# A four-layer hybrid kernel: first image requested ahead of the weights, first chunk's entry with one transfer behind its last step, first head's keys requested beside the last convolution

## The chip, the core and the metric

The kernel runs on one core of one Trainium2 chip. A core has five engines that run side by side, each through its own list of instructions in order: TensorE (PE in the profile, with its weight loads shown apart as PEld), VectorE (DVE), ScalarE (ACT), GpSimd (POOL) and SyncE (SP), which here issues nearly all transfers. The transfers themselves run on 16 DMA engines. The metric is the device time of one execution in microseconds (us), as the median of several runs; lower is better.

## The reference

The input x is four images of 128 channels by 64 x 64 pixels, in fp32. Four layers follow, each added to its input.

```python
x = x + _L0_conv_ref(_gn(x), ...)      # group norm, two depthwise convolutions, a patch sort, a scan
x = x + _L1_conv_ref(_gn(x), weight, bias)   # group norm, a 3x3 convolution of 128 to 128 channels
t = _to_tokens(x)                      # 4096 tokens of 128 channels per image
t = t + _L2_attn_ref(_ln_t(t), ...)    # attention with 16 heads of 8, then a small feed-forward
t = t + _L2_ffn_ref(_ln_t(t), ...)     # 64 experts
t = t + _L3_attn_ref(_ln_t(t), ...)    # linear attention
t = t + _L3_ffn_ref(_ln_t(t), ...)     # 64 experts
```

Layer 0 is what most of the change touches. Its core, for one image:

```python
feat = _gelu(_dwconv2d(x, conv1_w)); feat = feat * channel_gate(feat)
feat = _gelu(_dwconv2d(feat, conv2_w))
order = argsort of a score per 4x4 patch            # 256 patches
x1 = x[order] + pe[order];  x1n = layernorm(x1)     # 4096 positions in sorted order
xm, z = split(x1n @ in_proj_w.T)
xc = silu(causal convolution of 4 taps over xm)
dt = softplus(low-rank projection of xc)
h[t] = exp(dt * A) * h[t-1] + dt * B[t] * xc[t];  y[t] = sum over 16 states of h * C[t]
out = ((y + D * xc) * silu(z)) @ out_proj_w.T, put back at the original positions
```

In layer 2's attention the queries and keys of a head are the same 8 numbers, products of cosines of the normalised tokens, and the softmax runs over all 4096 tokens.

## The kernel before

**Layers 0 and 1** are written in `layers01` (line 284). It begins by requesting all weights on SP: eight small columns and matrices, then z_projT, conv1d_b, dt_projT, dt_b, the eight strided pieces of A_log, d_skip, out_projT, taps (the weights of layer 1), bias, x_projT, in_projT and taps1d, and the six pieces of the depthwise weights (`deep_t`). Some small products of weights follow on DVE and ACT, among them `taps1d * in_projT` (line 349) and `a_neg = -exp(A_log)` (lines 352 and 353).

`in_order(b)` (line 440) then prepares one image: it loads the image in four parts (`image`, line 397), takes the group norm's statistics (`groupnorm_scale`, line 177), writes the normalised image with a border into `xp`, stores `xp` to DRAM, and gathers it back in the layout that the depthwise convolution needs, eight rows at a time (`gather`, line 462: three transfers into a tile `under`, of which there are two). The first convolution's result `fp` is stored and gathered in the same way for the second. Scores per patch are sorted into ranks, the position rows `pe` are requested and added, each chunk of 512 positions is centred into `xn`, and `scaled_by_root` (line 678) multiplies it by the inverse deviation: TensorE spreads the deviations into PSUM, ACT copies them to `rs`, and POOL multiplies the two halves. Transposes and products with a permutation matrix give the sorted sequence `xq`.

For image 0 this runs alone (line 1050), in numbered slots: a slot is one step of the generator, and `K.slot` is its number. Outside the scan and the attention stages, a planner sets the order of each engine's instructions: it simulates the engines and, whenever one comes free, gives it the earliest-written instruction whose inputs and buffer are ready.

`scan` (line 736) walks over the four images in 32 chunks of 512 positions; its order is written out by hand for all engines, SP included. `enter(n)` (line 754) prepares chunk n while chunk n-1 is scanned. It computes xc, the projections and dt; `twice` (line 815) sends a tile through four transfers so that each 64 channels stand on both halves of the partitions. The last steps before the change are POOL's `e - u`, POOL's `dt + e`, `twice(dt2, dt)`, POOL's `dtx = dt * xc` and `twice(dtx2, dtx)`. Chunk 0's entry runs alone, before the scan's first step. Beside the scan of one image, `in_order` of the next image runs; beside the last, layer 0's end and layer 1 for the first three images. An operation given to `later` is issued at the next `K.flush`.

After the scan, `last()` (line 1084) does layer 0's end and layer 1 for image 3: `put_back`, group norm, and the 3x3 convolution in 16 pieces, some 50 steps.

**Layer 2** (`layer2_attention`, line 1128) has for each image a `prepare` (line 1243): eight chunks of 512 tokens through six stages (`fetch`, `centred`, `norm`, `products`, `running`, `store`), 48 steps; `store` writes the head values to `head_d` and `value_d` in DRAM. `loads` (line 1331) then asks for the keys and queries of head 0 with 32 transfers from `head_d` and casts both on POOL. `attention` (line 1344) follows, with the order on PE, DVE and POOL written by hand. For image 0, `prepare` runs step for step beside `last()`, and the loads run after both:

```python
part, l0_pools = before
run(part, stages)
l0_pools.close()
two = open_(left, "l2_two", 2)
run(loads(two))
```

`run` (line 1123) takes one step from each of its parts in turn until all are done. For images 1 to 3, `run(one_by_one(stages, loads(two)), *feed_forward(...))` (line 1728) already runs the loads behind `prepare`, beside the feed-forward of the image before. SBUF pools are opened from two ends, `left` and `right`, like stacks.

**Layers 2 and 3's experts and layer 3's attention** come after and are not touched.

Of the kernel before, what the change touches and what calls it, by code (L numbers as in the profile page):

```python
# [17 lines left out]
P = 128  # L18
NB = 4
# [264 lines left out]
def layers01(K, xd, dpool, w, w1):  # L284
# [14 lines left out]

    norm_g = column(nc, cst, w["norm_g"], "norm_g")  # L300
# [8 lines left out]
    z_projT = matrix(nc, cst, w["in_proj_wT"][:, 256:512], "z_projT")  # L309
    conv1d_b = column(nc, cst, w["conv1d_b"], "conv1d_b", 2)  # L310
    dt_projT = matrix(nc, cst, w["dt_proj_wT"], "dt_projT")
    dt_b = column(nc, cst, w["dt_proj_b"], "dt_b", 2)

    a_neg = cst.tile([P, NQ, NG], F32, name="a_neg")
    for z in range(2):
        for q in range(NQ):
            nc.sync.dma_start(
                out=a_neg[64 * z : 64 * z + 64, q, :].unsqueeze(2),
                in_=w["A_log"][64 * q : 64 * q + 64, :].rearrange("d (g z) -> d g z", z=2)[:, :, z : z + 1],
            )  # L320
    d_skip = column(nc, cst, w["D"], "d_skip", 2)
    out_projT = matrix(nc, cst, w["out_proj_wT"], "out_projT", 2)
    taps = cst.tile([P, 9, P], F32, name="taps")
    nc.sync.dma_start(out=taps, in_=w1["weightT"])
    bias = column(nc, cst, w1["bias"], "bias")

    x_projT = cst.tile([P, 2, 80], F32, name="x_projT")
    nc.vector.memset(x_projT, 0.0)
    for at, rows_ in ((0, slice(0, 24)), (64, slice(24, 40))):
        nc.sync.dma_start(  # L330
            out=x_projT[:, :, at : at + rows_.stop - rows_.start],
            in_=w["x_proj_wT"].rearrange("(k p) f -> p k f", k=2)[:, :, rows_],
        )

# [10 lines left out]
    in_projT = small.tile([P, 256], F32, name="in_projT", tag="rank_eq")  # L345
    nc.sync.dma_start(out=in_projT, in_=w["in_proj_wT"][:, 0:256])
    taps1d = cst.tile([P, 4, 256], F32, name="taps1d")
    nc.sync.dma_start(out=taps1d, in_=w["conv1d_wT"].partition_broadcast(P))
    nc.vector.tensor_tensor(
        taps1d, taps1d, in_projT.unsqueeze(1).to_broadcast([P, 4, 256]), ALU.mult  # L350
    )
    nc.scalar.activation(a_neg, a_neg, AF.Exp)
    nc.vector.tensor_scalar(a_neg, a_neg, -1.0, None, ALU.mult)
# [43 lines left out]
    def image(b):  # L397
        t = big.tile([P, L], F32, name="xb", tag="mid")
        src = w["x"][b].rearrange("c h w -> c (h w)")
        for q in range(4):  # L400
            at = slice(q * L // 4, (q + 1) * L // 4)
            nc.sync.dma_start(out=t[:, at], in_=src[:, at])
        return t

# [35 lines left out]
    def in_order(b, made, work, psum):  # L440
# [3 lines left out]
        xb = image(b)  # L444
# [17 lines left out]
        def gather(i, c):  # L462
            n = 8 * (HW + 2)
            t = unders[c] = work.tile([96, 4, n], F32, name="under", bufs=2)
            for ky in range(3):
                at = (8 * c + ky) * (HW + 2)
                nc.sync.dma_start(
                    out=t[32 * ky : 32 * ky + 32],
                    in_=image_d[i][:, at : at + n].rearrange("(g q) f -> q g f", q=32),
                )  # L470
# [207 lines left out]
        def scaled_by_root(n):  # L678
# [5 lines left out]
            def taken():  # L684
                rs = work.tile([P, CH], F32, name="ln_rs", tag="rs", bufs=1)
# [50 lines left out]
    def scan(seqs, others, work, psum, psbc, psex, psy):  # L736
# [17 lines left out]
        def enter(n):  # L754
# [49 lines left out]
            dt2, dtx2 = (work.tile([P, NQ, CH], F32, name=name) for name in ("dt2", "dtx2"))  # L804

# [16 lines left out]

            yield
# [7 lines left out]
            later(nc.gpsimd.tensor_tensor, e, e, u, ALU.subtract)  # L831
            yield
            later(nc.gpsimd.tensor_tensor, dt, dt, e, ALU.add)
# [1374 lines left out]
```

## Time and profile before

| | |
|---|---|
| median of 3 runs | 9565.78 us (9564.62 to 9581.03) |
| profiled execution | 9578.96 us, span of its instructions 9577.2 us |
| busy share of the span | PE 90%, DVE 75%, ACT 76%, POOL 52% |
| TensorE's mean granted clock | 0.934 of full speed |
| image 0's first scan begins | 234.82 us |
| scan of four images ends | about 2637 us |
| first score of image 0's attention | 2824.01 us |

The profile's times count from the start of the span. "L402" is line 402 of the kernel. A timeline row gives start, duration, engine, line, operation, the tile written and the tiles read, and how many instructions are merged in the row; in brackets stands how long the engine had idled before it and what released it. "SPq" rows are SP's requests for transfers; their duration is that of the issuing, not of the transfer. In a table of windows, each row gives the busy time of the engines in one stretch, TensorE's granted clock, the mean busy share of the 16 DMA engines and the rate in GB/s. An idle engine costs nothing unless what it waits for lies on the path that sets the end.

### The profile page before, as it was taken

What the parts mean: (1) busy time and instruction counts of PE and PEld (TensorE: products, weight loads), DVE (VectorE), ACT (ScalarE), POOL (GpSimd) and SP (SyncE); (2) the same over time, 40 slices, a digit from 0 to 9 for tenths busy, and PEclk for the clock granted to TensorE, in tenths of its full rate; (3) what the DMA queues carried; (4) which work ended last, traced back from release to release, by engine and by line L of the source; (5) the groups of instructions that cost most, each with busy time, mean ns of one, the idle gap of its engine ahead of it and who ended that gap; (6) DMA issues with size and microseconds to landing.
All of it is one profiled execution on the core that took longest, in us unless ns stands there. A gap on an engine that the chain in (4) does not pass through costs nothing.

```text
span 9577.2 us, 189161 instructions
## 1 busy us (share of the span) xinstructions
PE 8608.8 (90%) x74394; PEld 3287.8 (34%) x74394; DVE 7159.3 (75%) x7845; ACT 7287.0 (76%) x10505; POOL 4933.0 (52%) x3287
## 2 busy tenths in 40 slices
PE   5887888889879999979999979999989999998787
PEld 2221222234443333333333333333333333334444
DVE  1889798987858888868888867888876888874464
ACT  3776767654449999969999969999978999984232
POOL 1677676765525555555555545555555555543011
PEclk8887888889989999989999989999989999999998
DMA  4434425222232221141222233221222222231205
GB/s 118 122 77 109 108 72 128 74 67 80 71 86 39 39 41 40 32 112 40 40 40 40 39 94 55 38 41 39 39 81 62 40 40 40 40 97 58 81 10 168
DMA packets 580323, 631.22 MB, mean 66 GB/s; under 512 B 118816, under 2 KB 374888, under 8 KB 578536
## 3 DMA queue, kind: packets, MB, share of 16 engines
q1 hardware_dynamic: 579432, 619.12, 27.5%
q8 instruction: 586, 9.60, 0.4%
q14 instruction: 305, 2.50, 0.1%
HBM read 444.74 MB, written 106.97 MB: 58 GB/s over the span
## 4 chain that ended last, share of the span: by engine, by line
PE 60%; DVE 4%; DMA 2%; POOL 2%; issue 2%; ACT 2%; SPq 0%; DVEq 0%; POOLq 0%; ACTq 0%
PE ctx_ps L92 27%; PE acc_ps L92 14%; PE score L92 12%; PE ln_xc L92 1%; DMA w<-in_L_ffn_weight 1%; PE hid_ps L92 1%; PE kv L92 1%; POOL ln_sd L1845 1%; PE ln_var L129 1%; DVE ctx L1498 0%; DMA queries<-head_d 0%; POOL q L1293 0%; PE pool L92 0%; DVE x L1998 0%; ACT hid L1685 0%
## 5 line engine op out<-in xcount | busy, mean ns | idle before, releaser
L1564 ACT ACTIVATE ex<-score 128x1024 f32<-128x1024 f32 x5120 | 4924.1, 1038 | 235.8 <-PE score L92 147.9
L92 PE MATMUL ctx_ps<-ex,qt 128*32 128x512 f32 x20480 | 2733.2, 606 | 19.7 <-DVE ctx L1498 19.7
L1513 POOL TENSOR_TENSOR folded<-ex 128x1024 f32<-128x1024 f32 x512 | 1223.3, 2389 | 2100.3 <-ACT ex L1564 1826.9
L1570 DVE STREAM_TRANSPOSE turned<-ex 128x1024 f32<-128x1024 f32 x1536 | 1885.3, 1227 | 337.1 <-ACT ex L1564 336.8
L1546 DVE STREAM_TRANSPOSE turned<-ex 128x1024 f32<-128x1024 f32 x1532 | 1841.9, 1202 | 0.0
L92 PE MATMUL acc_ps<-turned,turned_v 128*32 128x256 f32 x24576 | 1769.3, 379 | 3.0 <-POOL qt L1251 2.3
L926 DVE TENSOR_TENSOR_SCAN hs<-decay,carry,hs 128x512 f32<-128x512 f32 x1024 | 1245.4, 1265 | 196.9 <-ACT decay L922 183.8
L92 PE MATMUL score<-queries,keys 32*128 32x512 f32 x10240 | 1334.3, 497 | 51.9 <-POOL queries L1241 47.0
L92 PEld LDWEIGHTS acc_ps<-turned,turned_v 128*32 128x32 f32 x24576 | 800.8, 110 | 1476.6 <-issue 1324.4
L930 POOL TENSOR_TENSOR hs<-hs,c_sb 128x1024 f32<-128x1024 f32 x512 | 1207.0, 2357 | 70.4 <-DMA c_sb<-c_d 31.4
L922 ACT ACTIVATE decay<-dt,a_neg 128x512 f32<-128x512 f32 x1024 | 693.0, 689 | 659.8 <-DVE hs L926 649.8
L92 PEld LDWEIGHTS score<-queries,keys 32*128 32x128 f32 x10240 | 512.4, 182 | 1145.7 <-ACT ex L1564 777.7
L1370 POOL TENSOR_TENSOR turned_v<-v,quarter 128x1024 f32<-128x1024 f32 x256 | 612.9, 2395 | 264.8 <-PE acc_ps L92 222.5
L92 PE MATMUL y_ps<-hs,pair 128*64 128x512 f32 x2048 | 656.1, 769 | 32.2 <-POOL hs L930 32.2
L1514 POOL TENSOR_TENSOR quarters<-folded 128x512 f32<-128x512 f32 x512 | 657.6, 1284 | 40.1
L92 PEld LDWEIGHTS ctx_ps<-ex,qt 128*32 128x32 f32 x20480 | 406.4, 108 | 655.2 <-issue 599.1
L915 DVE TENSOR_TENSOR hs<-dtx,b_ps 128x2048 f32<-128x2048 f32 x256 | 579.8, 2265 | 54.9 <-PE b_ps L92 31.0
L92 PE MATMUL b_ps<-dbc,state 32*64 32x512 f32 x1024 | 340.8, 747 | 237.4 <-DVE hs L915 237.3
L929 POOL COPY carry<-hs 128x2 f32<-128x2 f32 x512 | 97.9, 191 | 688.3 <-DVE hs L926 659.6
L1564 ACT ACTIVATION_READ_ACCUMULATOR ex<-score 128x1 f32 x2048 | 439.0, 214 | 0.0
L1498 DVE COPY ctx<-ctx_ps 128x512 f32<-128x512 f32 x256 | 176.8, 691 | 329.3 <-PE ctx_ps L92 317.8
L1555 DVE TENSOR_REDUCE dacc<-quarters 128x2 f32<-128x512 f32 x508 | 326.9, 643 | 0.0
(376 smaller groups left out, 8785.0 us busy)
## 6 DMA issues: line engine op xcount, KB each, us to landing
c_sb<-c_d SPq DMA_DIRECT2D x512, 128.0 KB
keys<-head_d SPq DMA_DIRECT2D x1024, 64.0 KB
queries<-head_d SPq DMA_DIRECT2D x1024, 64.0 KB
under<-image_d SPq DMA_DIRECT2D x192, 264.0 KB
dt<-dt SPq DMA_DIRECT2D x128, 256.0 KB
dtx<-dtx SPq DMA_DIRECT2D x128, 256.0 KB
v<-value_d SPq DMA_DIRECT2D x1024, 32.0 KB
w<-in_L_ffn_weight SPq DMA_DIRECT2D x32, 1024.0 KB
```

The source lines that it names most:

```text
L92: self.nc.tensor.matmul(out, lhsT, rhs, start=start, stop=stop)
L915: nc.vector.tensor_tensor(hs, dtx2, bb.unsqueeze(1).to_broadcast([P, NQ, CH]), ALU.mult)
L922: nc.scalar.activation(ex, dt2[:, q, :], AF.Exp, scale=a_neg[:, q, g : g + 1])
L926: nc.vector.tensor_tensor_scan(hs[:, q, :], decays[q - 2 * i], hs[:, q, :], carry[:, g, q : q + 1], ALU.mult, ALU.add)
L930: nc.gpsimd.tensor_tensor(hs[:, two, :], hs[:, two, :], cs.unsqueeze(1).to_broadcast([P, 2, CH]), ALU.mult)
L1370: nc.gpsimd.tensor_tensor(t, v.unsqueeze(2).to_broadcast([P, 4 * BT, 4, HD]), quarter.unsqueeze(1).to_broadcast([P, 4 * BT, 4, HD]), ALU.mult,
L1513: nc.gpsimd.tensor_tensor(hs, exs[:, :, 0], exs[:, :, 1], ALU.add)
L1514: nc.gpsimd.tensor_tensor(qs, hs[:, :, 0 : CH // 2], hs[:, :, CH // 2 :], ALU.add)
L1546: nc.vector.transpose(*upright)
L1555: nc.vector.tensor_reduce(at, qs, AX.X, ALU.add)
L1564: nc.scalar.activation(ex, sps[p], AF.Exp, scale=scale, accum_out=sums[:, t : t + 1] if summed else None)
L1570: nc.vector.transpose(*upright)
```

## The change

It has six parts, in the order of the program.

- Image 0 is requested first of all, before any weight. Twelve weights' loads (20 transfers) and their products move from the beginning into image 0's `in_order`, after slot 34; the exponential and negation of `a_neg` are written after slot 84.
- For image 0, `under` has four buffers in place of two.
- For image 0, `scaled_by_root` multiplies with two DVE operations straight from PSUM; the ACT copy and the two POOL products are gone.
- For chunk 0, `dtx2` is first filled with `xc` by `twice`; the two small POOL steps run on DVE; and once `dt2` has arrived, four DVE products make `dtx2 = dtx2 * dt2` in place. The second `twice` at the end is gone.
- `prepare` has two `x_in` buffers in place of three for image 0.
- The pool of keys and queries is opened on the right side, before `prepare`, for images 0 to 3. For image 0 the loads are put behind `prepare`'s stages, and this sequence takes two steps for each step of `last()`.

```diff
+    def image(b):
+        t = big.tile([P, L], F32, name="xb", tag="mid")
...
+    images = {0: image(0)}
+
     norm_g = column(nc, cst, w["norm_g"], "norm_g")
...
-    z_projT = matrix(nc, cst, w["in_proj_wT"][:, 256:512], "z_projT")
-    conv1d_b = column(nc, cst, w["conv1d_b"], "conv1d_b", 2)
-    dt_projT = matrix(nc, cst, w["dt_proj_wT"], "dt_projT")
...
-    nc.scalar.activation(a_neg, a_neg, AF.Exp)
-    nc.vector.tensor_scalar(a_neg, a_neg, -1.0, None, ALU.mult)
...
-        xb = image(b)
+        xb = images.pop(b) if b in images else image(b)
...
-            t = unders[c] = work.tile([96, 4, n], F32, name="under", bufs=2)
+            t = unders[c] = work.tile([96, 4, n], F32, name="under", bufs=2 if b else 4)
...
             def taken():
+                if b == 0:
+                    for a in range(2):
+                        nc.vector.tensor_tensor(inner(n, a), inner(n, a), outer(bp, a), ALU.mult)
+                    return
                 rs = work.tile([P, CH], F32, name="ln_rs", tag="rs", bufs=1)
...
+            light = nc.gpsimd if n else nc.vector
...
+            if n == 0:
+                twice(dtx2, xc)
             yield
...
-            later(nc.gpsimd.tensor_tensor, e, e, u, ALU.subtract)
-            yield
-            later(nc.gpsimd.tensor_tensor, dt, dt, e, ALU.add)
+            later(light.tensor_tensor, e, e, u, ALU.subtract)
+            yield
+            later(light.tensor_tensor, dt, dt, e, ALU.add)
             later(twice, dt2, dt)
             yield
-            later(nc.gpsimd.tensor_tensor, dtx, dt, xc, ALU.mult)
-            later(twice, dtx2, dtx)
+            if n:
+                later(nc.gpsimd.tensor_tensor, dtx, dt, xc, ALU.mult)
+                later(twice, dtx2, dtx)
+            else:
+                for q in range(NQ):
+                    later(nc.vector.tensor_tensor, dtx2[:, q], dtx2[:, q], dt2[:, q], ALU.mult)
...
-        for K.slot, _ in enumerate(in_order(0, seqs, work, psum)):
+        turns = enumerate(in_order(0, seqs, work, psum))
+        for K.slot, _ in turns:
             K.flush()
+            if K.slot == 34:
+                break
+        z_projT = matrix(nc, cst, w["in_proj_wT"][:, 256:512], "z_projT")
...
+        for K.slot, _ in turns:
+            K.flush()
+            if K.slot == 84:
+                nc.scalar.activation(a_neg, a_neg, AF.Exp)
+                nc.vector.tensor_scalar(a_neg, a_neg, -1.0, None, ALU.mult)
         K.flush()
...
-                xs[c] = work.tile([P, CH], F32, name="x_in", bufs=3)
+                xs[c] = work.tile([P, CH], F32, name="x_in", bufs=3 if b else 2)
...
-                if b == NB:
+                if b < NB:
+                    two = open_(right, "l2_two", 2, side="right")
+                else:
                     xs = images()
...
-                        run(part, stages)
+                        stages = one_by_one(stages, loads(two))
+                        run(part, stages, stages)
                         l0_pools.close()
-                        two = open_(left, "l2_two", 2)
-                        run(loads(two))
                     elif b < NB:
-                        two = open_(left, "l2_two", 2)
                         run(one_by_one(stages, loads(two)), *feed_forward(b - 1, past, work, psum))
```

More of the change, by code (lines that the diff above doesn't have):

```diff
@@ L298, in layers01 @@
     small = pool("l0_small", 1)
+    def image(b):
+        t = big.tile([P, L], F32, name="xb", tag="mid")
+        src = w["x"][b].rearrange("c h w -> c (h w)")
+        for q in range(4):
+            at = slice(q * L // 4, (q + 1) * L // 4)
+            nc.sync.dma_start(out=t[:, at], in_=src[:, at])
+        return t
+    images = {0: image(0)}
     norm_g = column(nc, cst, w["norm_g"], "norm_g")
@@ L308, in layers01 @@
     nc.vector.tensor_scalar(head_b, head_b, 0.5, None, ALU.mult)
-    z_projT = matrix(nc, cst, w["in_proj_wT"][:, 256:512], "z_projT")
-    conv1d_b = column(nc, cst, w["conv1d_b"], "conv1d_b", 2)
-    dt_projT = matrix(nc, cst, w["dt_proj_wT"], "dt_projT")
[L312 to L333, printed above, removed]
     row32 = K.shifted("row32_0", K.row_i, 1, (31, None, ALU.bitwise_and))
@@ L343, in layers01 @@
     nc.vector.tensor_tensor(pair, K.ident[:, 0:64], K.ident[:, 64:128], ALU.add)
[L345 to L351, printed above, removed]
-    nc.scalar.activation(a_neg, a_neg, AF.Exp)
-    nc.vector.tensor_scalar(a_neg, a_neg, -1.0, None, ALU.mult)
     head_bc = cst.tile([P, 64], F32, name="head_bc")
@@ L395, in layers01 @@
         nc.vector.tensor_scalar(befores[h], K.col, K.row[:, h : h + 1], None, ALU.is_gt)
[L397 to L403, printed above, removed]
     def staged(n, period, *stages):
@@ L1049, in layers01 @@
     ):
-        for K.slot, _ in enumerate(in_order(0, seqs, work, psum)):
+        turns = enumerate(in_order(0, seqs, work, psum))
+        for K.slot, _ in turns:
             K.flush()
+            if K.slot == 34:
+                break
+        z_projT = matrix(nc, cst, w["in_proj_wT"][:, 256:512], "z_projT")
+        conv1d_b = column(nc, cst, w["conv1d_b"], "conv1d_b", 2)
+        dt_projT = matrix(nc, cst, w["dt_proj_wT"], "dt_projT")
+        dt_b = column(nc, cst, w["dt_proj_b"], "dt_b", 2)
+        a_neg = cst.tile([P, NQ, NG], F32, name="a_neg")
+        for z in range(2):
+            for q in range(NQ):
+                nc.sync.dma_start(
+                    out=a_neg[64 * z : 64 * z + 64, q, :].unsqueeze(2),
+                    in_=w["A_log"][64 * q : 64 * q + 64, :].rearrange("d (g z) -> d g z", z=2)[:, :, z : z + 1],
+                )
+        d_skip = column(nc, cst, w["D"], "d_skip", 2)
+        out_projT = matrix(nc, cst, w["out_proj_wT"], "out_projT", 2)
+        taps = cst.tile([P, 9, P], F32, name="taps")
+        nc.sync.dma_start(out=taps, in_=w1["weightT"])
+        bias = column(nc, cst, w1["bias"], "bias")
+        x_projT = cst.tile([P, 2, 80], F32, name="x_projT")
+        nc.vector.memset(x_projT, 0.0)
+        for at, rows_ in ((0, slice(0, 24)), (64, slice(24, 40))):
+            nc.sync.dma_start(
+                out=x_projT[:, :, at : at + rows_.stop - rows_.start],
+                in_=w["x_proj_wT"].rearrange("(k p) f -> p k f", k=2)[:, :, rows_],
+            )
+        in_projT = small.tile([P, 256], F32, name="in_projT", tag="rank_eq")
+        nc.sync.dma_start(out=in_projT, in_=w["in_proj_wT"][:, 0:256])
+        taps1d = cst.tile([P, 4, 256], F32, name="taps1d")
+        nc.sync.dma_start(out=taps1d, in_=w["conv1d_wT"].partition_broadcast(P))
+        nc.vector.tensor_tensor(
+            taps1d, taps1d, in_projT.unsqueeze(1).to_broadcast([P, 4, 256]), ALU.mult
+        )
+        for K.slot, _ in turns:
[3 more added lines that the diff above has]
+                nc.vector.tensor_scalar(a_neg, a_neg, -1.0, None, ALU.mult)
         K.flush()
```

## The prediction

> **What bounds the kernel now.** I read the page first. TensorE is busy 90% of the span and makes 60% of the chain that ended last, nearly all of that in the attention stages (ctx_ps, acc_ps, score), which the change does not edit. So whatever it brings must come from stretches where no engine is full. I looked for those with the table of windows: the head of the program, before the scan, and the gap between the scan and the first attention. (Below: the chain's shares by engine; then stretch and length, busy us and count of PE, PEld, DVE, ACT, POOL, granted clock, DMA share, GB/s.)
>
> ```profile
> PE 60%; DVE 4%; DMA 2%; POOL 2%; issue 2%; ACT 2%; SPq 0%; DVEq 0%; POOLq 0%; ACTq 0%
> ...
> 10.00:20.00 10.00, 0.00 (x0) 0.00 (x0) 0.61 (x6) 2.80 (x3) 0.00 (x0) 1.00 0.66 142
> ...
> 2790.00:2810.00 20.00, 0.00 (x0) 0.00 (x0) 0.00 (x0) 0.00 (x0) 1.89 (x1) 0.53 0.62 66
> ```
>
> In both windows all compute engines are nearly still while DMA runs. The timeline says what they wait for (start, duration, engine, line, operation; in brackets the idle time and its releaser):
>
> ```profile
> 19.62 2.39 SPq L402 DMA_DIRECT2D xb<-in_x  x4
> 23.37 1.29 DVE L183 BATCH_NORM_STATS2 gn_st<-xb 128x6 f32<-128x512 f32 x2 [0.42 <-DMA xb<-in_x]
> 33.75 5.75 ACT L230 ACTIVATE xp<-xb,gn_off,gn_rs 128x512 f32<-128x512 f32 x8 [0.43 <-DVE gn_off L215]
> 35.33 4.51 SPq L458 DMA_DIRECT2D image_d<-xp  x4
> 46.84 8.72 PE L92 MATMUL conv<-under,deep 96*32 96x512 f32 x48 [13.82 <-DMA under<-image_d]
> 58.16 2.78 PE L92 MATMUL conv<-under,deep 96*32 96x512 f32 x24 [2.60 <-DMA under<-image_d]
> 90.64 4.73 PE L92 MATMUL conv<-under,deep 96*32 96x512 f32 x24 [2.33 <-DMA under<-image_d]
> ```
>
> The image is requested only at 19.62, behind every weight, and the chain (statistics, normalised image, store, gather, convolution) starts there. The first convolution then stalls between gathers.
>
> ```profile
> 172.10 1.66 POOL L691 TENSOR_TENSOR xn<-xn,ln_rs 128x256 f32<-128x256 f32 x2 [0.69 <-ACT ln_rs L686]
> 173.81 1.54 PE L716 MATMUL perm_t<-ident,xn 128*128 128x128 f32 x6 [8.96 <-POOL xn L691]
> ...
> 213.73 1.22 DVE L144 TENSOR_TENSOR dt<-sp_u,dt 128x1024 f32<-128x1024 f32 x1 [22.04 <-ACT dt L144]
> 220.61 2.95 SPq L818 DMA_DIRECT2D dt<-dt  x4
> 223.66 3.46 SPq L818 DMA_DIRECT2D dtx<-dtx  x4
> 232.43 2.29 DVE L915 TENSOR_TENSOR hs<-dtx,b_ps 128x2048 f32<-128x2048 f32 x1 [16.71 <-DMA dtx<-dtx]
> ```
>
> Here two serial chains: rows scaled by an ACT copy and two POOL products a chunk, and the first chunk's entry, which ends in two transfers one behind the other; the scan starts at 234.82.
>
> ```profile
> 2780.75 0.38 SPq L1323 DMA_DIRECT2D head_d<-part  x1
> 2787.78 11.97 SPq L1233 DMA_DIRECT2D keys<-head_d  x16
> 2800.19 15.15 SPq L1233 DMA_DIRECT2D queries<-head_d  x16
> 2822.06 1.89 POOL L1241 CAST queries<-queries 128x2048 fp32r<-128x2048 f32 x1 [12.25 <-DMA v<-value_d]
> 2824.01 1.51 PE L92 MATMUL score<-queries,keys 32*128 32x512 f32 x6 [37.30 <-POOL queries L1241]
> ```
>
> The last convolution ends at 2786.7 and TensorE idles 37.30 us for 32 small transfers that nothing covers.
>
> **The change part by part.** The profiled execution took 9578.96 us (span 9577.2, 1.76 around it), 13.2 above the median of the three runs shown, 9565.78. I sum what is saved on the profiled execution and take it from the median.
>
> *Image first.* SP's first request goes out at 0.74; the image's four (2.39 us) now stand there, ahead of 8 column loads, 6 deep_t loads, the 20 moved weight loads (4.48 to 15.85: 11.4 us of issuing) and two pe loads (1.40). From image request to first fill took 33.75 − 19.62 = 14.1, so the fill could begin at 14.9. Against it: DVE's constants (5.71 to 10.42, 4.7 us) wait for head_w and head_b, which now land later, and can lie ahead of the statistics: 19.6. The first store follows a fill by 1.6 (35.33 − 33.75): 16.5 to 21.2. SP itself is busy until 0.74 + 2.39 + 3.7 + 3.67 + 11.4 + 1.40 = 23.3 if all weights go first. So the store moves from 35.33 to between 16.5 and 23.3. I take 14 us saved (12 to 19), near the SP end, because the planner draws instructions without dependencies forward: pe is asked for after both convolutions in the code and goes out at 22.05. The same row says the weights, though placed in the middle of the first convolution, will go out early, in the 11.8 us that SP waited for the fill (queue waits: L458 on ACT xp, 14.8 in 4 times). If that cover is gone, 11.4 us of issuing stands between two gathers; I keep 3 as the low end of this term. Moved with them: taps1d's product (DVE 1.23), a_neg's negation (0.18), x_projT's memset (0.19), a_neg's exponential with its table load (ACT 0.23 + 1.28, and 1.28 to go back): beside the idle of both engines nothing, else at most 2.8.
>
> How late the columns are, this trace does not show. Its nearest row is head_w, released 2.2 us after its request with little ahead of it. The Trainium skill, "DMA: Bandwidth & Descriptors", section "Queues, rings and completion order", says each DMA engine takes its descriptors in ring order, which speaks against putting 2 MB ahead of the columns. By it the columns would land behind the image, at about 10 us, and the constants would follow: the 19.6 above; by the row alone 14.9. Both lie inside the range that SP's issuing already sets.
>
> *Four gather buffers.* No instruction is added. First convolution: 46.84 to 85, of which 8 × 2.78 = 22 are matmuls. DMA share was 0.45, 0.81, 0.80, 0.72 in the windows 47–52, 52–58, 67–72 and 72–78, so 2.75 + 1.1 + 1.0 + 1.7 = 6.5 us of transfer time were lost waiting for a buffer; elsewhere it is at 1.0, which no buffer changes. Second convolution: its first gather was issued at 86.12, after the first had ended, and its matmuls began at 90.64; with free buffers it can be there by 86: 4.5. Together at most 11; I take 9 (3 to 13, with 2 for a warmer clock: that row took 4.73 against 2.78).
>
> *Scaling on DVE.* Removed: 8 ACT copies (0.58) and 16 POOL products (0.83). Added: 16 DVE products from PSUM; nearest rows 0.48 (xb<-conv) and 0.62 (xb<-xb,perm_p, also strided), upper bound POOL's 0.83. A chunk then costs 1.25 instead of a cycle of 2.35. After the last root (160.77) four chunks remain: 160.8 + 0.4 + 4 × 1.25 = 166.2 instead of 173.76, saving 7.6 (5.9 to 8.7); POOL no longer alternates with the pe additions, whose matmuls waited 2.3 + 3.9 us: take 1.4. Sum 9 (6 to 12).
>
> *Entry of chunk 0.* dtx2 is filled with xc early: four DMAs (3 us of SP) behind c_d, in SP's 14.8 us wait for POOL dt. POOL's two steps (2.34 each) become DVE (1.22 each): dt done at 215.7 + 2.45 = 218.15. dt2's transfer needed 7.04 us from first request to the last decay's release (220.61 to 227.65): 225.2. Then three of four products of 128x512 (half of 1.22, so 0.64) and the 2.29 product: scan at 229.5 instead of 234.82, 5 saved (4 to 6).
>
> *Keys beside the last convolution.* prepare's stages now take two steps for each of the last image's steps, followed by the 32 loads; chunk buffers x_in 2 for 3, free, since no ln_xc row there waits for x_in and an answer of some 2 us (head_w's) is asked a chunk (8 us or more) ahead. Two ends compete. Loads: DVE work per chunk is 0.30 + 0.17 + 4 × 0.69 + 0.41 + 7 × 0.31 + 0.23 + 0.69 = 6.7; 8 chunks 54, plus putting back (16 × 0.62) and statistics (6.7): 71 from 2662; at full use store 7 is at 2733, at 80% at 2751. From that store to the cast queries took 41.3 (2780.75 to 2823.95, less 2 in which SP stood behind the xd store): 2774 to 2792. Convolution: began 2701.2 with half of prepare ahead of it; the other half (27 us of DVE) may now lie ahead: I take half of that, start 2715, 16 × 4.05 = 65 and 8 of leftover prepare matmuls: 2788 (2766 to 2801). On SP the xd stores queue behind the loads, and only the end of the stage waits for them. Attention's buffers may lie over xb, whose last store lands some 3 later. First score about 2793 instead of 2824.01: 30 saved (19 to 47). In later attention stages only the pool's place moves: nothing, bounded in the third rival.
>
> **Sum:** 14 + 9 + 9 + 5 + 30 = 67. 9565.78 − 67 = 9499. Low ends 3 + 3 + 6 + 4 + 19 = 35: 9531; high ends 19 + 13 + 12 + 6 + 47 = 97: 9469.
>
> **The rivals.**
> *The convolution waits instead.* If all 27 us of DVE work, and the in-order waits behind it, hold back the statistics, TensorE ends the convolution near 2815 and the gap only moves. For it: DVE was already busy 16.4 of 20 us at 2680–2700. Against: TensorE was busy just 7.8 there, and idle time can be filled. Saved 37: 9529.
> *Transfers bound the head.* DMA share is 1.01 at 40–47 and 58–62; gathers and image stores could simply fill the same engines, and the weights' 1.6 MB with them. Then four buffers save nothing and the image 12 at most: 67 − 9 − 2 = 56, and with the weights between gathers 45: 9510 to 9521.
> *Slower: the moved working set.* The keys' pool on the right moves the attention's buffers, in all four stages. 5120 exponentials take 1033 ns (1014 to 1157 seen); from 17 ns more each (87 us) the kernel is slower by over 0.2%: 9585. For it: ACT is 9 tenths full there, so any loss shows. Against: the same neighbours in a shifted place, and the median sits within 2% of the minimum.
>
> **How the numbers follow.** Forecast 62 in 100, convolution waits 17, transfers bound 10, slower 7; 4 for gains that cancel. The measurement tells about 0.2% (19 us) from no change; the first three cases are all faster by more. So faster 0.88, same 0.04, slower 0.08. The forecast's own range is 9476 to 9524, since five terms seldom end at one side together; with the rivals on the fast side 9470 to 9536, which leaves the slower cases out.
>
> **What would show it.** Right: xb requested before 2 us; first fill before 20; conv rows a steady 3 to 4 us apart before 75; no POOL xn rows in the head; first scan near 197; first score within 6 us of the last conv. Wrong: weight loads between two gathers; conv starting after 2725; a score row released by queries again; ACTIVATE ex above 1050 ns.

## The result

The changed kernel takes 9539.94 us (median of 8 runs, 9515.23 to 9551.72); the kernel before took 9575.08 us beside it (8 runs, 9560.02 to 9581.53). The ratio is 0.9961 (95% interval 0.9951 to 0.9972): 35 us faster by the medians. The forecast was 9499, range 9470 to 9536, so the direction was right and the size was not: about half of the 67 us came. The profiled execution took 9539.78 us, its span 9538.0, against 9577.2 before.

First the shares of the chain that ended last, from the page after the change, and then two of its windows (stretch, length, then busy us and count of PE, PEld, DVE, ACT and POOL, granted clock, DMA share, GB/s):

```profile
PE 60%; DVE 4%; POOL 2%; issue 2%; DMA 2%; ACT 1%; SPq 0%; DVEq 0%; POOLq 0%; ACTq 0%
```

```profile
10.00:20.00 10.00, 1.17 (x4) 1.00 (x4) 5.39 (x28) 4.42 (x7) 0.00 (x0) 1.00 0.37 86
...
2748.23:2778.23 30.00, 28.79 (x136) 24.40 (x134) 3.87 (x8) 0.00 (x0) 3.78 (x2) 1.00 0.55 113
```

The first window, nearly empty of work before, now holds the last statistics, the group norm's chain and the first fills; in the second, TensorE works for 28.79 of the 30 us around the attention's first score, ahead of which it used to sit still for 37.30. So both idle stretches named in the prediction are filled. What they turned into stands in the timeline (start, duration, engine, line, operation; in brackets idle time and releaser). Here is one row of the kernel before (its channel average), and then the head after the change:

```profile
85.74 0.16 DVE L524 TENSOR_REDUCE favg<-fsum 128x1 f32<-128x8 f32 x1 [52.03 <-ACT fp L144]
...
0.73 1.82 SPq L305 DMA_DIRECT2D xb<-in_x  x4
15.84 5.75 ACT L230 ACTIVATE xp<-xb,gn_off,gn_rs 128x512 f32<-128x512 f32 x8 [0.42 <-DVE gn_off L215]
17.45 4.49 SPq L425 DMA_DIRECT2D image_d<-xp  x4
29.01 13.16 PE L92 MATMUL conv<-under,deep 96*32 96x512 f32 x96 [13.89 <-DMA under<-image_d]
43.42 6.26 SPq L1041 DMA_DIRECT2D a_neg<-in_L_conv_A_log  x5
54.28 0.43 SPq L1062 DMA_DIRECT2D taps1d<-in_L_conv_conv1d_wT  x1
54.83 4.94 SPq L434 DMA_DIRECT2D under<-image_d  x6
61.37 1.31 SPq L434 DMA_DIRECT2D under<-image_d  x2
64.47 7.35 PE L92 MATMUL conv<-under,deep 96*32 96x512 f32 x48 [10.80 <-DMA under<-image_d]
72.71 0.34 SPq L425 DMA_DIRECT2D image_d<-fp  x1
73.10 6.76 SPq L434 DMA_DIRECT2D under<-image_d  x10
77.55 5.06 PE L92 MATMUL conv<-under,deep 96*32 96x512 f32 x24 [2.46 <-issue]
152.62 0.87 PE L687 MATMUL perm_t<-ident,xn 128*128 128x128 f32 x6 [2.73 <-DVE xn L654]
202.07 0.69 DVE L144 TENSOR_TENSOR dtx<-dtx,dt 128x512 f32<-128x512 f32 x1 [5.82 <-DMA dt<-dt]
207.63 4.81 DVE L904 TENSOR_TENSOR_SCAN hs<-decay,carry,hs 128x512 f32<-128x512 f32 x4
```

The image store begins 17.9 us earlier (35.33 to 17.45), and so does the first matmul (46.84 to 29.01). Then the lead shrinks: from 43.42 to 54.7 SP requests weights, the next gather is asked only at 54.83, and TensorE waits 10.80 us in the middle of the first convolution. That ends (channel average on DVE) at 72.71 against 85.74, 13.0 earlier. The lead is nearly unchanged through the second convolution (12.8 behind it), grows by 8.4 in the scaling (last transpositions 173.81 to 152.62), by 0.8 in the stretch between, and by 5.2 in chunk 0's entry (from its first product, 22.0 earlier), and the scan starts at 207.63 against 234.82: 27.2 us earlier.

The boundary between the scan and image 0's attention, first three rows of the kernel before and then the rows after the change:

```profile
2673.94 0.50 PE L985 MATMUL perm_t<-ident,xq 128*128 128x128 f32 x3
2701.19 2.04 PE L92 MATMUL conv<-xp,taps 128*128 128x256 f32 x4
2825.01 2.86 ACT L1564 ACTIVATE ex<-score 128x1024 f32<-128x1024 f32 x3 [45.84 <-PE score L92]
...
2648.23 0.50 PE L963 MATMUL perm_t<-ident,xq 128*128 128x128 f32 x3
2702.93 1.91 PE L92 MATMUL conv<-xp,taps 128*128 128x256 f32 x4
2738.93 11.89 SPq L1252 DMA_DIRECT2D keys<-head_d  x16
2764.99 11.97 SPq L1000 DMA_DIRECT2D xd<-xb  x4
2769.93 1.89 POOL L1260 CAST queries<-queries 128x2048 fp32r<-128x2048 f32 x1 [9.47 <-DMA xd<-xb]
2776.02 1.15 PE L92 MATMUL score<-queries,keys 32*128 32x512 f32 x6
2779.84 1.28 ACT L1583 ACT_TABLE_LOAD   x1 [56.49 <-DMA xd<-xb]
2781.14 2.85 ACT L1583 ACTIVATE ex<-score 128x1024 f32<-128x1024 f32 x3
2782.21 1.71 PE L92 MATMUL score<-queries,keys 32*128 32x512 f32 x4 [5.05 <-ACT ex L1583]
```

I measure this stretch from the last transposition row of `put_back` (2673.94 before, 2648.23 after) to the first exponential (2825.01 and 2781.14). It has three pieces: to the convolution's first matmul, the convolution, and from its end to the exponential.

| us | to the convolution | convolution | to the exponential | sum |
|---|---|---|---|---|
| before | 27.25 | 85.56 | 38.26 | 151.07 |
| after | 54.70 | 73.09 | 5.12 | 132.91 |

The loads are fully covered (queries cast at 2771.8, convolution's end at 2776.0), and the gap behind the convolution gave back 33.1 us. But the convolution starts 27.4 us later, and only 12.5 of that returns inside it. Net 18.2 us.

Front and boundary together: 27.2 + 18.2 = 45.4 us. In these two profiles 39.2 us of span remain, because the scan was 1.5 us longer and everything behind the first exponential 4.7 us longer. There the code is the same, but for the place of the pool of keys and queries, and the experiments show below how far such stretches scatter.

### The profile page after: what moved, and what is told of

Its sections match the earlier page's. It is cut to its first block, busy times and chain, and to the rows that moved or that the text cites. A ratio compares the mean times of both kernels' runs of the same rounds, so it can differ in the third digit from the quotient of the medians.

```text
span 9538.0 us, 189166 instructions
## 1 busy us (share of the span) xinstructions
PE 8615.8 (90%) x74394; PEld 3292.9 (35%) x74394; DVE 7170.9 (75%) x7867; ACT 7291.5 (76%) x10500; POOL 4913.6 (52%) x3268
## 4 chain that ended last, share of the span: by engine, by line
PE 60%; DVE 4%; POOL 2%; issue 2%; DMA 2%; ACT 1%; SPq 0%; DVEq 0%; POOLq 0%; ACTq 0%
PE ctx_ps L92 28%; PE acc_ps L92 14%; PE score L92 12%; PE ln_xc L92 1%; PE hid_ps L92 1%; PE kv L92 1%; DMA w<-in_L_ffn_weight 1%; PE conv L92 1%; POOL ln_sd L1864 1%; PE ln_var L129 0%; DVE ctx L1517 0%; DVE x L2017 0%; PE pool L92 0%; POOL q L1312 0%; PE ans_ps L92 0%
## 5 line engine op out<-in xcount | busy, mean ns | idle before, releaser
L1583 ACT ACTIVATE ex<-score 128x1024 f32<-128x1024 f32 x5120 | 4927.4, 1037 | 184.1 <-PE score L92 98.4
L92 PE MATMUL score<-queries,keys 32*128 32x512 f32 x10240 | 1333.0, 497 | 16.5 <-ACT ex L1583 7.9
```

The lines of the kernel that those rows point to most:

```text
L92: self.nc.tensor.matmul(out, lhsT, rhs, start=start, stop=stop)
L1583: nc.scalar.activation(ex, sps[p], AF.Exp, scale=scale, accum_out=sums[:, t : t + 1] if summed else None)
```

## The experiments

All are edits of the changed kernel, save one (the boundary alone). The markers are the channel average, the first scan and the boundary's sum above (us), and each ratio is against runs of the kernel before on the same chip; the first line is the kernel before as it ran beside the change. In the expectations a "turn" of the front is what the code calls a slot.

| | channel average | first scan | boundary | time (median) | ratio to before, 95% |
|---|---|---|---|---|---|
| before | 85.74 | 234.82 | 151.07 | 9575.08 | |
| change | 72.71 | 207.63 | 132.91 | 9539.94 | 0.9961 [0.9951, 0.9972] |
| change again | 71.95 | 207.43 | 129.80 | 9525.14 | 0.9944 [0.9931, 0.9956] |
| front alone | 71.59 | 206.88 | 151.62 | 9549.19 | 0.9963 [0.9950, 0.9975] |
| boundary alone | 87.33 | 239.09 | 132.63 | 9562.57 | 0.9985 [0.9976, 0.9994] |
| weights on ACT's queue | 73.21 | 209.75 | 132.53 | 9528.43 | 0.9952 [0.9937, 0.9967] |
| few bytes | 69.01 | 206.32 | 133.02 | 9518.7 (one run) | |
| weights at slot 42 | 64.84 | 205.22 | 129.67 | 9523.01 | 0.9951 [0.9939, 0.9964] |
| two buffers | 78.24 | 214.58 | 132.72 | 9546.35 (one run) | |
| one to one for 24 steps | 75.73 | 212.31 | 122.03 | 9524.10 | 0.9956 [0.9939, 0.9972] |
| one to one throughout | 73.55 | 208.79 | 146.36 | 9552.79 | 0.9978 [0.9968, 0.9987] |
| slot 42 and 24 steps | 64.89 | 206.13 | 123.90 | 9522.56 | 0.9946 [0.9933, 0.9960] |
| slot 52, 24 steps, three to one | 61.30 | 197.81 | 126.01 | 9523.33 | 0.9937 [0.9923, 0.9951] |
| slot 52, 24 steps, two to one | 61.55 | 198.31 | 121.53 | 9518.19 | 0.9942 [0.9928, 0.9955] |

### Where the first convolution lost its lead

The first suspicion was the thirteen requests between two gathers. One run sent all twenty over ACT's queue, in the way shown here for one; another kept the requests and cut the bytes, loading with `little` only one column of the five largest weights.

```diff
-            nc.sync.dma_start(
+            nc.scalar.dma_start(
```

> The changed kernel, with the 20 moved weight transfers requested on ACT's queue in place of SP's; the order then has all 20 ahead of ACT's first activation and none between the gathers. Theory (the weights that went out between two gathers, 43.42 to 54.83, cost the head about 10 us): the 10.80 us that TensorE stood before 64.47 fall below 3, the channel mean (favg, 72.71) comes at 60 to 64, the first scan at 195 to 200 instead of 207.63, and the whole is 7 to 12 us faster than the changed kernel, about 0.995 of before. Rival (the first convolution is bound by its own gathers and stores on the DMA engines, whatever the weights do): favg stays within 3 us of 72.71 and the time within 3 us of the changed kernel.

```diff
-        taps = cst.tile([P, 9, P], F32, name="taps")
-        nc.sync.dma_start(out=taps, in_=w1["weightT"])
+        taps = little(cst.tile([P, 9, P], F32, name="taps"), w1["weightT"])
```

> The changed kernel with the same requests at the same places on SP, but z_projT, out_projT, taps, in_projT and taps1d bring one column each (the rest of these tiles is zero), so 1.4 MB of weights are not moved and the computation leaves them out. It tells the two ways apart in which the weights could hold the gathers. If it is SP's issuing (11.4 us between two gathers): TensorE's gap of 10.80 us stays at 8 or more. If it is the bytes on the DMA engines: the gap falls below 5 and favg comes 5 to 8 us earlier.

On ACT's queue the convolution itself did what was expected: 48.1 us from first fill to average in place of 56.9, no wait over 3.57 us. But the average came at 73.21, not 60 to 64, and the scan at 209.75. (That the average lies within 3 us of the change's is the rival's number, but not for the rival's reason.) ACT asked at once, and the first fill began at 25.08 instead of 15.84:

```profile
15.17 0.34 SPq L261 DMA_DIRECT2D head_w<-in_L_conv_head_w  x1
18.37 0.26 DVE L330 TENSOR_SCALAR head_bc<-ones,head_w 128x64 f32<-128x64 f32 x1 [3.45 <-DMA head_w<-in_L_conv_head_w]
25.08 5.75 ACT L230 ACTIVATE xp<-xb,gn_off,gn_rs 128x512 f32<-128x512 f32 x8 [2.70 <-DVE gn_off L215]
```

The loss had moved upstream. Beside ACT's requests SP took 6.12 us to ask for the image (1.82 in the change) and came to head_w only at 15.17 (7.20). DVE stood 3.45 us for it ahead of the group norm's aggregate (18.54, in the change 12.79), and then had products of the weights in its order ahead of the norm's last steps. Only some 2 of the 9.2 us are the image's own: its third pair of statistics began at 9.42 instead of 7.21. The Trainium skill, "DMA: Bandwidth & Descriptors", section "Issuing engines are not separate DMA queues", says that transfers asked by different engines interleave on the same 16 DMA engines; these 2.2 us agree with it; the rest came from the issuing and from DVE's order.

With few bytes the wait was 7.53 us in place of 10.80 and the average 69.01: neither theory's numbers (at least 8, or below 5). Five builds with the change's front have the average at 71.6 to 75.7, 2.6 to 6.7 us later than this one run. The rows of the few-bytes run show how the two parts divide:

```profile
54.58 3.10 SPq L434 DMA_DIRECT2D under<-image_d  x6
61.06 7.06 PE L92 MATMUL conv<-under,deep 96*32 96x512 f32 x48 [7.53 <-DMA under<-image_d]
```

The gather is asked as late as in the change (54.58 and 54.83), as the same requests stand ahead of it, but its first matmul comes 6.5 us behind the request and not 9.6. So the issuing holds the gather back, which is most of the wait, and the bytes then lengthen it by some 3 us.

Then the requests were put at slot 42, behind the first convolution's last gather, in SP's order.

```diff
-            if K.slot == 34:
+            if K.slot == 42:
```

> The only edit: the twenty weight requests are written at turn 42 of image 0's front instead of turn 34, which puts them in SP's order behind the last gather of the first convolution and ahead of the last store of its output. Theory 'requests between the gathers': the first convolution shrinks from the 56.9 us between first fill and channel average in the changed kernel to the 48.1 us measured with the requests on ACT's queue, with the fill still near 16: average at 63 to 66 us (72.71 in the changed kernel), no PE wait over 4 us between two of its rows, first scan at 197 to 201 us (207.63), some 8 us off the changed kernel, about 0.995 of the kernel before. Rival 'moved on': the twenty now hold back the last store and the second convolution's gathers instead; average at 63 to 66, but the first scan at 205 to 209 and the time that of the changed kernel, about 0.996. Rival 'bytes': not the place but the 1.6 MB beside the gathers costs the time; then the average comes at 68 or later.

The average came at 64.84, as the first theory has it, but the scan at 205.22, as "moved on" has it. The timeline of this kernel shows where the loss went:

```profile
55.23 3.53 SPq L1041 DMA_DIRECT2D a_neg<-in_L_conv_A_log  x5
64.83 0.33 SPq L425 DMA_DIRECT2D image_d<-fp  x1
65.25 9.86 SPq L434 DMA_DIRECT2D under<-image_d  x12
73.68 5.35 PE L92 MATMUL conv<-under,deep 96*32 96x512 f32 x24 [5.28 <-DMA under<-image_d]
```

The weights are being moved while the second convolution's first gather should be: it starts 8.8 us after the average, where the change needs 4.8, so 4.0 of the 5.5 us that the scan lost against the average are lost there. The last store itself was not held back, as SP was through with the weights at 63.57. But none of the first gather's three requests stands ahead of that store any more (in the change two do). At slot 52, fifteen of the second convolution's gather requests stand ahead of the weights. That kernel was run in two variants, with the boundary's pace altered too; the diff shows the three-to-one variant, and the other keeps the change's own `run(part, stages, stages)` as its last line. The taps' product (1.23 us on DVE, which does nothing else from 54.80 to 64.50 in the changed kernel) moves to slot 64, its old place goes:

```diff
+            if K.slot == 64:
+                nc.vector.tensor_tensor(
+                    taps1d, taps1d, in_projT.unsqueeze(1).to_broadcast([P, 4, 256]), ALU.mult
+                )
...
+                        run(islice(part, 24), islice(stages, 24))
-                        run(part, stages, stages)
+                        run(part, stages, stages, stages)
```

> Two edits on the changed kernel. The weight requests at turn 52, behind fifteen of the second convolution's gathers, with the product of the taps written at turn 64; and at the boundary 24 turns one to one, then three turns of preparing to one of the last convolution. Theory 'requests must stand where four buffers are already full': channel average 63 to 66 us, the second convolution's first matmul within 6 us of it (4.8 in the changed kernel, 8.8 and 11.8 with the requests at turn 42), first scan at 195 to 199 us (207.63 in the changed kernel, 205.22 with turn 42). Rival 'moved on again': the rows of the second convolution wait instead, first scan at 203 or later. At the boundary, theory 'the last convolution is over and the head's loads are late' (2:1 after turn 24 gave 122.0 and 123.9 us from the last put-back transposition to the first exponential): 115 to 120 us. Rival 'the preparing takes the convolution's place on DVE again': 124 or more. Time some 20 us under the changed kernel, 0.994 of the kernel before.

> The changed kernel with the weight requests at turn 52 (the taps' product at turn 64), and at the boundary 24 turns one to one and then the change's own two to one. Theory 'each gain holds by its marker': channel average 60 to 63 us, first scan 196 to 199, first exponential 121 to 124.5 us behind the last put-back transposition (three to one gave 126.0: there the preparing held the convolution up again), together 19 us under the changed kernel (10 at the front, 10 at the boundary), 0.993 of the kernel before (0.992 to 0.9945). Rival 'the pace after turn 24 makes no difference': 125 or more.

The head of the two-to-one variant:

```profile
46.75 10.61 PE L93 MATMUL conv<-under,deep 96*32 96x512 f32 x72 [3.88 <-DMA under<-image_d]
61.54 0.34 SPq L426 DMA_DIRECT2D image_d<-fp  x1
61.94 11.21 SPq L435 DMA_DIRECT2D under<-image_d  x13
66.49 5.35 PE L93 MATMUL conv<-under,deep 96*32 96x512 f32 x24 [2.57 <-DMA under<-image_d]
73.19 7.17 SPq L1042 DMA_DIRECT2D a_neg<-in_L_conv_A_log  x5
198.31 4.81 DVE L905 TENSOR_TENSOR_SCAN hs<-decay,carry,hs 128x512 f32<-128x512 f32 x4
```

The same thirteen requests (seven again go out early) now hold nobody up: four full buffers feed TensorE while SP is at them. The average comes at 61.55, the scan at 198.31 and, in the other variant, 197.81. The prediction's 197 was there to be had; the place of the weights took 9 us of it. The boundary's pace, changed in the same runs, comes after the scan and can't be the reason.

The buffers were tested by taking two of the four away:

```diff
-            t = unders[c] = work.tile([96, 4, n], F32, name="under", bufs=2 if b else 4)
+            t = unders[c] = work.tile([96, 4, n], F32, name="under", bufs=2)
```

> The changed kernel with two gather buffers for image 0 instead of four, all else kept. Theory 'the buffers bring nothing while the weights' requests stand between the gathers': channel average at 71 to 75 us (72.71 with four), first scan 206 to 210, the time that of the changed kernel. Rival, the prediction's step, 'four buffers are worth 3 to 13 us': average at 76 to 85, first scan at 211 to 220.

```profile
68.98 8.37 PE L92 MATMUL conv<-under,deep 96*32 96x512 f32 x48 [11.00 <-DMA under<-image_d]
78.24 0.16 DVE L491 TENSOR_REDUCE favg<-fsum 128x1 f32<-128x8 f32 x1 [11.46 <-ACT fp L144]
```

My theory that the buffers bring nothing fell: the average came at 78.24, 5.5 us later than in the change (2.5 to 6.7 later than the five builds with its front), and the scan at 214.58, 7.0 later. The four buffers bring about as much with the weights between the gathers as without. From fill to average: two buffers without weights between the gathers 52.0 us (the kernel before), two with them 62.4, four with them 56.9, four without 45.5 (slot 52).

### Where the boundary lost its gain

First, each half of the change by itself. The boundary alone is the kernel before with the last part of the diff; the front alone is the change without it.

> The kernel before with only the change's part at the boundary: the head's loads chained behind the preparing, two turns of preparing to each turn of the last convolution's part, two input buffers, the buffers for keys, queries and values on the right side. First scan stays at 235 us. Theory 'the full 27 us of preparing stand ahead of the convolution': the first exponential 131 to 135 us behind the last put-back transposition (151.1 before, 132.9 in the changed kernel), 18 us saved, 0.9981 of the kernel before (0.997 to 0.999). The prediction's step, 30 us: the first exponential 121 us behind, 0.9969. Rival 'the boundary's gain hangs on the earlier front': less than 10 us, over 0.999.

> The changed kernel with its boundary part undone (part and preparing one to one, loads after, three input buffers, the buffers for keys, queries and values on the left side). Theory 'the two halves add': first scan 206 to 210 as in the changed kernel, the first exponential 150 to 152 us behind the last put-back transposition as in the kernel before, 27 us saved, 0.9972 of the kernel before (0.9962 to 0.9982); with the boundary alone (0.9985) that makes the change's 0.9961. Rival 'one hides the other': the front alone saves 35 or more, or under 15.

By the markers both hold: 132.63 us for the boundary alone against 132.91, and for the front alone the scan at 206.88 with a boundary of 151.62. The halves don't lean on each other. One marker missed: with the boundary alone the scan began at 239.09, not 235, though the code ahead of it is that of the kernel before. In time the front alone saved 32 us by the medians and 35 by the ratio, between the theory's 27 and its rival's 35, so the time doesn't decide. By the ratios, 0.9985 times 0.9963 is 0.9948.

Next, what costs the late start. If it is the preparing, taken at double pace from the first step, then a single pace until the convolution begins must bring it back, and a single pace throughout must also bring back the gap.

```diff
+                        run(islice(part, 24), islice(stages, 24))
                         run(part, stages, stages)
```

> The changed kernel, with layer 2's preparation taking one step per step of the last image for the first 24 steps (to the end of its group norm) and two after that. Theory (the double pace put preparation ahead of the group norm on DVE and ACT, which made the last convolution start 78.4 us after the first transposition of the put-back, where it was 51.3): it starts at 51 to 58 again, the keys are still covered or nearly, and the first exponential comes 138 to 148 us after that transposition instead of 156.6: 8 to 18 us faster than the changed kernel. Rival (the late start comes from two x_in buffers in place of three, or from the keys' pool): the convolution still starts later than 70, and the time stays within 4 us of the changed kernel.

```diff
-                        run(part, stages, stages)
+                        run(part, stages)
```

> The changed kernel, with one step of preparation and loads for each step of the last image, so that the loads only follow in the code. Theory: the convolution starts at 51 to 58 after the first transposition as before, preparation's last store comes near 130, and some 41 us of requests and casts stand bare behind it: first exponential at 165 to 178 instead of 156.6, 8 to 20 us slower than the changed kernel. Rival (the double pace brings nothing, the loads are drawn forward anyway): first exponential at 150 to 160, within 4 us of the changed kernel or faster.

| us | to the convolution | convolution | to the exponential | sum |
|---|---|---|---|---|
| change | 54.70 | 73.09 | 5.12 | 132.91 |
| one to one for 24 steps | 27.26 | 86.17 | 8.60 | 122.03 |
| one to one throughout | 27.25 | 85.40 | 33.71 | 146.36 |
| slot 52, 24 steps, two to one | 27.28 | 86.38 | 7.87 | 121.53 |
| slot 52, 24 steps, three to one | 27.27 | 88.61 | 10.13 | 126.01 |

Both came as expected, and the rival is out, since two input buffers and the pool's new place are in both runs: the doubled pace delays the start by all of its 27 us, and without the delay the boundary gives 29.0 us. Chaining the loads alone gives 4.7. How the start is held shows in the group norm's short chain, from the aggregate of the statistics to the reciprocal of the deviation and the first fill of the convolution's input (xp). In the changed kernel:

```profile
2676.91 0.36 DVE L187 BATCH_NORM_AGGREGATE gn_mv<-gn_st 128x2 f32<-128x48 f32 x1
2693.38 0.16 DVE L214 RECIPROCAL gn_rs<-gn_sd 128x1 f32<-128x1 f32 x1
2701.59 0.81 ACT L230 ACTIVATE xp<-xb,gn_off,gn_rs 128x512 f32<-128x512 f32 x1
```

and with 24 steps one to one:

```profile
2667.96 0.36 DVE L188 BATCH_NORM_AGGREGATE gn_mv<-gn_st 128x2 f32<-128x48 f32 x1
2674.81 0.13 DVE L215 RECIPROCAL gn_rs<-gn_sd 128x1 f32<-128x1 f32 x1
2675.17 1.52 ACT L231 ACTIVATE xp<-xb,gn_off,gn_rs 128x512 f32<-128x512 f32 x2 [1.76 <-DVE gn_off L216]
2767.05 1.89 POOL L1261 CAST queries<-queries 128x2048 fp32r<-128x2048 f32 x1 [7.25 <-DMA xd<-xb]
2769.00 1.47 PE L93 MATMUL score<-queries,keys 32*128 32x512 f32 x6 [6.70 <-DMA v<-value_d]
```

From the last transposition to the aggregate it takes 28.7 and 19.1 us, and the chain from there to the reciprocal, whose instructions take some 2.4 us, 16.5 and 6.9: its steps stand in DVE's, ACT's and PE's order behind the preparing's. Together that is 19 of the 27 us. The other 8 are the first fill's own wait on ACT: it comes 8.2 us behind the reciprocal in the changed kernel and 0.4 with the single pace.

With the start restored, the loads end the stage: 32 requests of 0.7 to 0.9 us each on SP, two casts, and TensorE idles 5.8 to 6.9 us ahead of the first score. (The score's row above names v, but the queries' cast ends at 2768.94, just ahead of it.) Three to one was meant to draw the loads forward and shorten the stage, and did the opposite: 126.01, as its rival had it. Ahead of the score, 6.87 us of waiting remained, and the convolution grew by 2.2.

### Both together, and the scatter

> Two edits at once: the weight requests at turn 42, and the first 24 turns of the last convolution's part taken one to one with the preparing before the two-to-one pace begins. Theory 'both losses are separate': 8 us from the front and 11 from the boundary (the pace alone brought the first exponential from 132.9 to 122.0 us behind the last put-back transposition), 19 us off the changed kernel, 0.994 of the kernel before (0.993 to 0.995), first scan at 197 to 201, first exponential 121 to 124 us behind the last put-back transposition. Rival 'only one of them is on the path': 0.9950 or more.

> The changed kernel again, unaltered, beside the others of this call. Theory 'builds with the same code scatter by some 5 us and not more': first scan 206 to 210, first exponential 132 to 134 us behind the last put-back transposition, 0.9955 to 0.9968 of the kernel before. If it comes below 0.9953, the totals of the later variants (0.9946 to 0.9956) can't be told from the changed kernel, and only their markers can.

With slot 42 and the 24 steps the boundary kept its gain (123.90), the front did not (206.13, expected 197 to 201). The time fell inside the expected ratio, but that proves little, as the change measured again shows: 0.9944 where it had been 0.9961, some 16 us, so the theory of a scatter of 5 us fell. Its markers repeat the first ones within 0.8 us in the head and 3.1 at the boundary, while the stretch behind the first exponential was 6756.9 us in the one profile and 6766.9 in the other. Over all profiles that stretch goes from 6748.3 to 6766.9, and from first scan to last transposition from 2432.9 to 2443.3 (without the run that leaves weights out), with no order that follows the edits. So a difference in time under some 15 us between two builds is not told from scatter here, and I rest on the markers: 45 us for the change, which as a ratio is 1 − 45.4/9577.2 = 0.9953, the middle of its two measurements. The markers scatter too, if less: with the change's front the scan begins at 206.9 to 212.3 us in five builds, with the front of before at 234.8 and 239.1, and with the change's boundary the sum is 129.7 to 133.0 in seven. The means of these builds give 28 us for the front and 19 for the boundary.

The last variant (slot 52, 24 steps, two to one) saves 36.5 us at the scan and 29.5 at the boundary, 66 in all by the markers, what the prediction asked of the change; of the spans 57 us remain. Its median, 9518.19 (9516.71 to 9521.55), is the lowest of all; its ratio, 0.9942, overlaps that of the change's second measurement, and its scan took 2443.3 us, the longest seen. That it beats the change is shown by the markers (20 us) and not by the ratio.

## Why the prediction was wrong

**Base.** I counted from the three runs' 9565.78; over more runs the kernel before has 9575, so 9 of the 41 us between 9499 and 9540 are the base. Of the other 32, 10 are the front (27.2 us for the 37 of its four terms), 12 the boundary, 6 the scatter of the profiled pair, and 4 the difference between that pair and the medians.

**Image first, 14: the failed step.** The store and the first matmul moved by 17.9, inside the range. What failed is "the weights, though placed in the middle of the first convolution, will go out early". I argued that from pe, requested at 22.05 though written late. But the planner gave SP only seven of the twenty ahead of the store; thirteen stood between the gathers, the first of the prediction's own signs of being wrong. The exact case was priced ("11.4 us of issuing stands between two gathers", low end 3) and then not taken. The two-buffer run sizes the term: average 7.5 us earlier than before, 17.9 less 10.4. The fill came at 15.84, near the 14.9 that the row gave and not at the 19.6 that went with the skill's ring order. But that order was not tested: the planner put the constants that need no column between the image's statistics (8.41 to 11.44), and the products of head_w and head_b only at 12.63 and 13.08.

**Four buffers, 9.** Worth 5.5 at the average (one run without them), inside 3 to 13. The 4.5 us expected in the second convolution did not come: it still starts 4.84 us after the average (4.90 before). Only two of its first gather's three requests stand ahead of the last store of `fp` (61.37 in the timeline); the third comes behind it at 73.10, and the store waits for the first convolution's end. A free buffer doesn't help there.

**Scaling 9, entry 5.** 8.4 and 5.2. The pair of DVE products took 1.12 us where 1.25 was taken.

**Keys beside the last convolution, 30: the second failed step.** 18.2. "I take half of that" was the error: all 27 us lay ahead. On the clock of the kernel before that is a start at 2728.6 where 2715 was taken, past the 2725 that the prediction named as a sign of being wrong. The loads were covered as forecast. The convolution's length (65 + 8 = 73) came out at 73.09, but by luck: in that stretch TensorE spent 66.9 us on the convolution and only 2.0 on other work, and stood idle for 4.2, which was not in the sum. The last store of xb, put at "some 3 later", cost 5.05 us of TensorE ahead of the second score.

**The rivals.** "The convolution waits instead" named the right mechanism and the wrong price: the start moved by the whole 27, yet the gap didn't merely move, since the convolution ran 12.5 us shorter without the preparing and the 33 us behind it vanished. Its 37 us in total is near the measured 35 only because its front was too good. "Transfers bound the head" was right in the part about weights between gathers (some 3 us of that loss are their bytes), and wrong about the buffers. "Slower" fell: the exponentials take 1037 ns against 1038, far from 1050.

## What to carry to other kernels

When loads are moved out of the way of a first request, find the place in the issuing queue, not in the code, where they'll stand, and ask what waits right behind them; the same thirteen requests cost 10 us between two gathers, moved the loss on at a second place, and were free where four buffers stood full. When background work is paired with a critical chain, start its faster pace only when the chain's short dependent steps are past: each waits in order on several engines, and here the background work ahead of it counted in full. And before a total is compared, measure one kernel twice: markers settled here what ratios could not.

## What was not expected of the hardware

The same request took longer to ask while the DMA engines were full. The strided pieces of A_log took 0.67 us each in the kernel before (8 in 5.38, DMA share 0.39 meanwhile), 1.25 between the gathers (5 in 6.26, share 1.10) and 1.43 at slot 52 (5 in 7.17, share 1.09). Slow issuing and full engines go together here; no run shows which causes which.

The first row of the second convolution meets half clock after the pause and takes 4.73 to 5.35 us instead of 2.78, and the row after it starts 8.0 us after the first in the kernel before, 8.3 in the change and 10.2 in the last variant. In windows of a quarter to half a microsecond, the granted clock there is 0.50 for 6.8 us in the kernel before (87.8 to 94.6) and in the change (75.4 to 82.2), for 10.2 us in both slot 52 variants, and for 17.1 us in both slot 42 variants: two, three and five times 3.41 us. The other builds have 6.8 or 10.2. The Trainium skill, "TensorE: Matmul & The Clock Gate", section "What's actually happening", says the gate opens after a busy window that runs freely and isn't restarted by the work; half-clock stretches that come in whole multiples agree with that. A longer stretch costs that row some 2 us here.
